# A two-layer relational graph convolution: node blocks of 256 instead of 512 in layer 1, a change of the gather table for each, and limits computed later

## The chip, the cores and the metric

The kernel runs on one core of a Trainium2 chip. The metric is device time in microseconds (us). Besides the timed runs there is one profiled execution, from which every view of the trace comes. Engines are named as in the profile: PE is TensorE (PEld its weight loads), DVE is VectorE, ACT is ScalarE, POOL is GpSimd, SP is SyncE. A "q" behind a name (SPq, ACTq, POOLq) is the engine's own queue, which issues DMAs and waits.

## The reference

12,500 nodes with 128 features each, and 200,000 edges, which come sorted by their destination node. An edge's type, one of 10, is the argmax of 10 of its 42 attributes. Each of two layers gathers the source rows, takes the mean for each pair of destination and type, multiplies it by the type's 128x128 matrix, and adds the root term and the bias:

```python
def _rgcn_layer(x, src, dst, edge_type, w_rel, root, bias):
    N = x.shape[0]
    seg = dst * NUM_REL + edge_type
    xs = x[src]
    sums = jax.ops.segment_sum(xs, seg, num_segments=N * NUM_REL)
    cnt = jax.ops.segment_sum(jnp.ones(seg.shape, x.dtype), seg, num_segments=N * NUM_REL)
    mean = (sums / jnp.maximum(cnt, 1.0)[:, None]).reshape(N, NUM_REL, -1)
    return jnp.einsum('nrd,rdo->no', mean, w_rel) + x @ root + bias
h = relu(_rgcn_layer(x, ..., w_rel1, root1, b1))
out = layernorm(x + _rgcn_layer(h, ..., w_rel2, root2, b2))
```

Layer 2 needs `h` of an edge's source, so in principle all of layer 1 comes first.

## The kernel before, in words

**Tiles, parts, blocks.** The edges are cut into NT = 1563 tiles of 128. Four tiles (QB) are a part; there are 391 parts. Layer 1 (`layer_1`, from L830) is one loop over the parts, its instructions in the order in which the Python code writes them (a manual schedule). For each tile POOL gathers 128 source rows by one indirect DMA (`gathered`, L747-750). DVE makes a one-hot matrix of 128 x 120 from the keys (`ones`, L757), ACT weights it (`weighted`, L752), PE multiplies it with the gathered rows (L976), and DVE adds the product to the sums `cc` (`sum_into`, L781) at a node offset that `offsets` loads from a row of limits, two parts later. `cc` is a ring over 1024 nodes for each layer. Since the edges are sorted, the sums of a block of nodes are complete after a certain tile, `done_after(k)`. Then `finish(k)` (L838) runs: `projected` (L730) multiplies the ten sums with the weight matrices on PE; one part later `rows_out` adds the bias, applies the relu (ACT) and turns the block on PE; two parts later `rows_kept` copies it to `hb` (ACT), and SP stores it to `hD`. `second` and `second_kept` write what the block already has of layer 2 to `T2`; `cleared` (L715) zeroes the ring; `fetch`, `turn` and `turned_kept` bring the next block's rows.

**The table.** From tile T0 = 166 on, a gather does not read `x` alone. It reads a row of `XH`, which is `x` beside `h`, if `h` is known for that node, and beside zero if not. So an edge whose source is in a finished block gets its layer 2 message in layer 1, at no further gather. There are two tables, `XH[0]` and `XH[1]`, used in turn. Blocks K0 to K1 (`KSEEN`, L49) each open an epoch: from a fixed tile on (`first_seen`, L124), a multiple of RT = 11 tiles behind T0 and at least READY = 6 parts after the part in which the block finishes, gathers read the other table, which holds this block too. `stored` (L743) writes the block's `hb` to the table that comes next, and, two parts into its epoch, to the other one (`todo_late`). `table_rows` (L819) fills the tables with `x` and zeros through the ACT queue, 13 pieces of 1024 rows for each table, at parts set in L931 to L934.

**Layer 2.** Edges whose source was not yet known are packed into NT2 tiles while layer 2 begins with tiles 0 to 165, which it gathers again from `hD`. `brought_together` (L1057) packs them, row by row: a row is 11 tiles, 1408 edges, and there are NR = 127 rows. How many places a row gets is fixed when the program is made: for a row whose epoch knows the nodes below b, 1408 x (1 - b/12500) plus 4.25 standard deviations (`groups`, `extents`, L131 to L147). `row_limits` (L386) puts b and the room of each row on the chip and `tile_limits` (L404) the nodes that a packed tile can reach; both are made of small DVE instructions and are only read in layer 2. Two walks over the packed tiles alternate, and layer 2 finishes its own blocks, the last of which ends the program.

**Buffers.** Gathers land in 7 buffers (GB). One holds 8 tiles while only `x` is gathered, 4 tiles with both halves from T0 on, and 8 tiles in layer 2. POOL can run that far ahead of PE.

**Prologue.** Before the loop the first 128 tiles' keys and weights are prepared. `places` (L350) computes each tile's node limit, in one DVE instruction for each block (L359), and `row_limits` is called there (L1033).

Of the kernel before, what the change touches and what calls it, by code (L numbers as in the profile page):

```python
# [20 lines left out]
P = 128  # L21
# [24 lines left out]
RT = 11  # L46
REACH = 560
SIGMAS = 4.25
KSEEN = (1, 21)  # L49
SPLIT = 63  # L50
LEAD = 40
LAST = 40
# [11 lines left out]
def rgcn_resnorm_kernel(ctx: ExitStack, tc: tile.TileContext, x, src, dst, attr, w_rel1, root1, b1,  # L64
# [16 lines left out]
    NPT = len(parts)  # L81
    CP = CT // QB
    NPAD = N + W
    starts = list(range(0, N - YB - 2 * P, YB))
    starts += list(range(starts[-1] + YB, N, P))
    lap = N // RN * RN
    assert lap in starts
    NBLK = len(starts)
# [261 lines left out]
    def places():  # L350
        off = keep.tile([NCH, CT], F32, name="off")
        early(0, nc.vector.tensor_tensor(off, b_i, even, op=ALU.subtract))
        b_f = keep.tile([NCH, CT], F32, name="b_f")
        lows = keep.tile([NCH, CT], F32, name="lows")
        early(0, nc.vector.memset(lows, 0.0))
        for size in (YB, P):
            for k in range(NBLK - 1):
                if done_after(k) < NT and starts[k + 1] - starts[k] == size:
                    early(0, nc.vector.scalar_tensor_tensor(lows, even, STEP * done_after(k) - 0.5, lows,  # L359
                                                            op0=ALU.is_gt, op1=ALU.add))  # L360
            if size == YB:
                early(0, nc.vector.tensor_scalar(lows, lows, float(YB // P), None, op0=ALU.mult))
# [12 lines left out]
        nc.vector.tensor_tensor(fl[:NCH], fl[:NCH], worst, op=ALU.max)  # L375
# [10 lines left out]
    def row_limits():  # L386

        nc.vector.memset(seen_below, float(starts[K0 + 1]))
        for i in range(3):
            nc.vector.memset(rooms[:, i:i + 1], float(groups[0][2 + i]))  # L390
        was_k, was = starts[K0 + 1], groups[0]
        for (k, r, _), now in zip(rows_of[1:], groups[1:]):
            more(seen_below, r, starts[k + 1] - was_k)
            for i in range(3):
                more(rooms[:, i:i + 1], r, now[2 + i] - was[2 + i])
            was_k, was = starts[k + 1], now

    NC2 = -(-NT2 // P)
    reach_of = [keep.tile([P, NC2], F32, name=f"reach{i}") for i in range(2)]
# [273 lines left out]
    def block_rows(a, k, l):  # L673
# [4 lines left out]
            nc.tensor.transpose(pr[:h, t, :], a[:, t * P:t * P + h], ident)  # L678
        if not l:
            nc.sync.dma_start(hT[:, n0:n0 + n], a[:, :n])  # L680
            hb = fin.tile([P, 4, C], F32, name="hb")
            for p, s in spans(k):
                nc.scalar.activation(hb[:p, s], pr[:p, s], AF.Copy)
            rows_dma(hb, hD, k, True)
# [145 lines left out]
    def layer_1():  # L830
# [2 lines left out]
        done = 0  # L833
        zps, ohs, xbs, fTs = {}, {}, {}, {}
        offs, row = None, None
        big = [k for k in range(NBLK) if block(k)[1] == YB]

        def finish(k, t):  # L838

# [21 lines left out]
            def rows_kept(_):  # L861
                pr = po.pop()
                hb = fin.tile([P, 4, C], F32, name="hb")
                for p, s in spans(k):
                    nc.scalar.activation(hb[:p, s], pr[:p, s], AF.Copy)
                rows_dma(hb, hD, k, True)
                if k <= K1:
                    first = 0 if k <= K0 else (k - K0) % 2
                    stored(hb, first, k)
                    if k < K1:  # L870
                        assert k <= K0 or t >= first_seen[k - 1]
                        when = t + 8 * QB if k < K0 else first_seen[k] + 2 * QB
                        todo_late.append((when, lambda t: stored(hb, 1 - first, k)))

# [14 lines left out]
                todo.at(t + 3 * u, lambda t: cleared(0, k, 1))  # L889
            if k < NBLK - 1:  # L890
                todo.at(t + (9 if k >= NBLK - 3 else 3) * u, second)
                todo.at(t + (9 if k >= NBLK - 3 else 5) * u, second_kept)
            else:
                todo.run(t)
                todo.run(END)
                todo.at(t, second)
                todo.at(t, second_kept)
            if both:
                w = 10 if k >= NBLK - 3 else 6
                todo.at(t + w * u, lambda t: cleared(1, k, 0))  # L900
                todo.at(t + (w + 1) * u, lambda t: cleared(1, k, 1))
            if k + 1 < NBLK - 1:
# [13 lines left out]
                    fTs[k + 1] = fin.tile([P, 4 * P], F32, name="fT")  # L916
                    nc.scalar.activation(fTs[k + 1][:, :n], pt[:, :n], AF.Copy)
                todo.at(t + u, fetch)
                w = 2 if k == NBLK - 3 else 5
                todo.at(t + w * u, turn)  # L920
                todo.at(t + (w + 1) * u, turned_kept)

# [4 lines left out]
        jobs = Later()  # L927
        for c in range(1, NCH):
            jobs.job(max(0, (c - 1) * CP - 3) * QB, prepared(c), QB)
        jobs.job(8 * QB, tile_limits(), 2 * QB)  # L930
        for b in range(2):  # L931
            for i, a in enumerate(range(0, N, 2 * YB)):
                n = i + b * 13
                jobs.at((1 + n * 3 // 2 if n < 22 else 1 + n * 2) * QB, lambda t, b=b, a=a: table_rows(b, a))  # L934
        for i, a in enumerate(range(0, NREL * RW, YB)):
            def wipe(t, a=a):
                m = min(YB, NREL * RW - a)
# [92 lines left out]
        pc = summed_up(0, same(0, kh, d), d, pc)  # L1030
    weights_out(0, weights_turned(0, [pc]))
    places()
    row_limits()  # L1033
    weights_in()
    in_order = ExitStack()
    in_order.enter_context(tc.manual_schedule())
# [652 lines left out]
```

## Time and profile before

| | us |
|---|---|
| median of 3 runs | 3094.66 (3094.16 to 3096.91) |
| the profiled execution's own time | 3098.4 |
| its span, first to last instruction | 3096.6 |
| gathers, all on POOL | 1397 from XH, 166 from x, 166 + 709 from hD |
| mean granted TensorE clock | 0.823 |

The page gives, for each group of instructions, the line, the engine, the operation and its operands, the count, the busy time, the mean of one in ns, and the idle time of the engine just before them with what ended it. "issue" there means that the profile shows nothing that the engine waited for. In views of windows each engine's busy time is followed by its count of instructions; behind them stand the granted clock, the busy share of the DMA engines and the GB/s. In a timeline a row has its start, its duration, the engine, the line and the operands.

### The profile page before, as it was taken

The numbers are of one execution on the slowest core, as the hardware profiler recorded it, in microseconds if no ns is written. First come the engines' busy times: TensorE is split into PE (matmuls) and PEld (weight loads), VectorE is DVE, ScalarE is ACT, GpSimd is POOL, SyncE is SP. The second block draws the span as 40 slices with busy tenths as digits, with TensorE's granted clock in tenths as the row PEclk, the third lists the DMA queues.
The fourth block names the chain that finished last, engine by engine and source line by source line (L and its number), as shares of the span: only waits on it lengthen the run. The fifth ranks groups of instructions, "written<-read, shape, count | busy, mean of one in ns | idle before, by whom it ended". The sixth has DMA issues, their size and how long they took to land.

```text
span 3096.6 us, 39943 instructions
## 1 busy us (share of the span) xinstructions
PE 2427.0 (78%) x10905; PEld 1805.4 (58%) x10905; DVE 1989.1 (64%) x5272; ACT 1292.9 (42%) x3006; POOL 2308.9 (75%) x2450
## 2 busy tenths in 40 slices
PE   2768887888888888888888899646577787777887
PEld 2546666566666566666666667545555555555665
DVE  7875746465656565555555554598677677677676
ACT  3543333333333333333333334322445555555453
POOL 7777777777777777777777777677777777777774
PEclk8768888888888878787888789856788999988888
DMA  7865445454545454545454444322222222222222
GB/s 210 233 204 173 143 124 159 120 163 123 163 119 163 121 162 124 162 123 162 123 161 124 127 121 120 101 58 63 60 70 74 73 74 74 74 74 73 74 73 59
DMA packets 260631, 371.57 MB, mean 120 GB/s; under 512 B 49654, under 2 KB 189467, under 8 KB 260404
## 3 DMA queue, kind: packets, MB, share of 16 engines
q0 software_dynamic: 100368, 251.49, 29.5%
q1 hardware_dynamic: 106339, 91.83, 9.6%
q10 hardware_dynamic: 53697, 25.62, 2.8%
q8 instruction: 94, 1.54, 0.2%
q14 instruction: 133, 1.09, 0.1%
HBM read 323.78 MB, written 57.76 MB: 123 GB/s over the span
## 4 chain that ended last, share of the span: by engine, by line
PE 37%; POOL 18%; issue 16%; DVE 13%; DMA 11%; ACT 3%; DVEq 1%; ACTq 0%; POOLq 0%; SPq 0%
POOL g L749 18%; PE pf L737 16%; DMA g<-XH,idxE 10%; PE zp L976 9%; PE zp L1479 8%; DVE cc L790 4%; DVE oh L766 2%; PE pf L740 1%; ACT cc L720 1%; ACT oh L755 1%; DVE cc L1157 1%; PE pf L1195 1%; DVEq L775 1%; DVE oh L763 1%; DVE go L1145 1%
## 5 line engine op out<-in xcount | busy, mean ns | idle before, releaser
L749 POOL DMA_INDIRECT g<-XH,idxE x1397 | 1321.7, 946 | 425.6 <-issue 383.9
L790 DVE TENSOR_TENSOR cc<-cc,zp 128x240 f32 (+16 forms) x2507 | 962.9, 384 | 719.7 <-PE zp L976 503.1
L976 PE MATMUL zp<-oh,g 128*128 128x120 f32 x5920 | 1053.4, 334 | 323.6 <-DMA g<-XH,idxE 230.5
L976 PEld LDWEIGHTS zp<-oh,g 128*128 128x128 f32 x5920 | 926.1, 236 | 482.4 <-issue 187.1
L749 POOL DMA_INDIRECT g<-hD,idxB x709 | 670.2, 945 | 216.1 <-issue 202.7
L755 ACT ACTIVATE oh<-oh,wE 128x120 f32<-128x120 f32 x1729 | 530.2, 383 | 640.8 <-DVE oh L763 557.3
L1479 PE MATMUL zp<-oh,g 128*128 128x120 f32 (+18 forms) x1888 | 514.8, 417 | 256.8 <-DVE cc L790 102.3
L737 PE MATMUL pf<-cc,w 128*128 128x256 f32 (+6 forms) x2120 | 691.4, 485 | 30.3 <-DVE cc L790 21.3
L1479 PEld LDWEIGHTS zp<-oh,g 128*128 128x128 f32 x1888 | 346.1, 230 | 401.8 <-issue 252.2
L737 PEld LDWEIGHTS pf<-cc,w 128*128 128x128 f32 x2120 | 411.8, 208 | 279.6 <-issue 205.0
L755 ACT ACTIVATE oh<-oh,wB 128x150 f32<-128x150 f32 (+18 forms) x778 | 342.6, 483 | 293.7 <-DVE oh L766 276.6
L766 DVE TENSOR_TENSOR oh<-go,keyB 128x480 f32<-128x480 f32 (+14 forms) x478 | 262.9, 550 | 132.8 <-PE zp L1479 131.6
L720 ACT ACTIVATE cc<-zero 128x2560 f32<-128x2560 f32 (+4 forms) x188 | 322.0, 1717 | 21.7 <-DVE cc L790 19.6
L763 DVE TENSOR_TENSOR oh<-bank,keyE 128x480 f32<-128x480 f32 x391 | 253.2, 648 | 0.0
L670 ACT ACTIVATE a<-pf,b 128x512 f32<-128x512 f32 (+1 forms) x27 | 17.3, 639 | 453.6 <-PE pf L740 453.6
L749 POOL DMA_INDIRECT g<-hD,idxE x166 | 158.4, 954 | 62.6 <-issue 46.6
L749 POOL DMA_INDIRECT g<-in_x_dram,idxE x166 | 157.0, 946 | 52.3 <-issue 47.2
L546 DVE TENSOR_TENSOR eqb<-bank,kh 128x1344 bf16<-128x1344 f32 (+2 forms) x65 | 100.5, 1549 | 2.3 <-PE pf L557 1.9
L555 PE MATMUL pf<-eqb,identb 128*128 128x512 bf16 (+2 forms) x130 | 64.7, 498 | 11.6 <-DVE eqb L546 11.4
L882 ACT ACTIVATE v<-pf,b 128x512 f32<-128x512 f32 (+2 forms) x29 | 18.0, 619 | 120.1 <-PE pf L740 100.5
L557 PE MATMUL pf<-eqb,identb 128*128 128x512 bf16 (+2 forms) x130 | 64.1, 493 | 0.0
L415 DVE SCALAR_TENSOR_TENSOR reach<-u,reach 128x6 f32<-128x6 f32 x252 | 42.2, 167 | 7.4
(235 smaller groups left out, 991.5 us busy)
## 6 DMA issues: line engine op xcount, KB each, us to landing
m<-in_edge_attr_dram SPq DMA_DIRECT2D x48, 672.0 KB
g<-XH,idxE POOLq DMA_INDIRECT x1397
XH<-in_x_dram ACTq DMA_DIRECT2D x24, 512.0 KB
XH<-zero ACTq DMA_DIRECT2D x24, 512.0 KB
g<-hD,idxB POOLq DMA_INDIRECT x709
XH<-hb SPq DMA_DIRECT2D x43, 256.0 KB
out_dram<-o SPq DMA_DIRECT2D x47, 128.0 KB
xb<-in_x_dram SPq DMA_DIRECT2D x23, 256.0 KB
```

Source lines behind the costliest of these rows:

```text
L546: nc.vector.tensor_tensor(eq[:p], kpP[:p, None, :R].to_broadcast([p, DB, R]), fore, op=ALU.is_equal)
L555: nc.tensor.matmul(pc[:p], identb[:p, :p], eq[:p, k:k + 4, L:], start=(d + k == 1), stop=False)
L557: nc.tensor.matmul(pc[:p], identb[:p, :p], back, start=False, stop=(d + k + 3 == L))
L720: nc.scalar.activation(cc[:, l, h * H:(h + 1) * H, o:o + n], zero[:, None, :n].to_broadcast([P, H, n]), AF.Copy)
L737: nc.tensor.matmul(po[:, :n], wsb[l][:, r, :], cc[:, l if ring is None else ring, r, o:o + n], start=(r == 0), stop=False)
L749: nc.gpsimd.indirect_dma_start(out=g[:, j * C:(j + n) * C], out_offset=None, in_=table, in_offset=bass.IndirectOffsetOnAxis(ap=idx, axis=0))
L755: nc.scalar.activation(s, s, AF.Copy, scale=w)
L763: nc.vector.tensor_tensor(o.rearrange("p (t m) -> p t m", m=m), cols[:, None, :m].to_broadcast([P, n, m]), keys[:, :, None].to_broadcast([ ...
L766: nc.vector.tensor_tensor(o.rearrange("p (t r n) -> p t r n", r=NREL, n=w), cols[:, None, :, :w].to_broadcast([P, n, NREL, w]), keys[:, :, ...
L790: nc.vector.tensor_tensor(s, s, z, op=ALU.add)
L976: nc.tensor.matmul(zp[:, a + l * KW:a + (l + 1) * KW], g[:, (slot[j] + l) * C:(slot[j] + l + 1) * C], oh[:, j * KW:(j + 1) * KW], start=Tr ...
L1479: nc.tensor.matmul(zp[:, j * m:(j + 1) * m], gt[:, b * C:(b + 1) * C], oh[:, j * m:(j + 1) * m], start=True, stop=True)
```

## The change

Blocks of layer 1 have 256 nodes instead of 512 (the last six stay at 128 and less). There are 52 instead of 29. Epochs are opened by blocks 3 to 43 instead of 1 to 21: the first still knows the nodes below 1024 and the last those below 11,264, but there are 41 instead of 21, and the known border moves by 256. `hb` becomes two buffers of half the size, in turn. The later steps of a finish move up by a part. `tile_limits` starts at part 80 instead of 8. `row_limits` leaves the prologue and becomes a job of the loop from part 180 on, eight DVE instructions every second part. The 26 pieces of the tables are issued at parts 1 + 3n/2 (rounded down) throughout; before, the last four of them stood at parts 45, 47, 49 and 51 (now 34, 35, 37 and 38). The second table's first piece comes second; the other pieces of the first table follow at once.

```diff
-KSEEN = (1, 21)
+BN = 2 * P
+KSEEN = (3, 43)
...
-    starts = list(range(0, N - YB - 2 * P, YB))
-    starts += list(range(starts[-1] + YB, N, P))
+    starts = list(range(0, N - YB - 2 * P, BN))
+    starts += list(range(starts[-1] + BN, N, P))
...
-        for size in (YB, P):
+        for size in (BN, P):
...
             was_k, was = starts[k + 1], now
+            yield 1
...
-                hb = fin.tile([P, 4, C], F32, name="hb")
+                hb = fin.tile([P, 2, C], F32, name=f"hb{k % 2}")
...
-                        assert k <= K0 or t >= first_seen[k - 1]
+                        assert k <= K0 or now + QB >= first_seen[k - 1]
...
-                todo.at(t + (9 if k >= NBLK - 3 else 5) * u, second_kept)
+                todo.at(t + (9 if k >= NBLK - 3 else 4) * u, second_kept)
...
-                w = 10 if k >= NBLK - 3 else 6
+                w = 10 if k >= NBLK - 3 else 5
...
-                w = 2 if k == NBLK - 3 else 5
+                w = 2 if k == NBLK - 3 else 4
...
-        jobs.job(8 * QB, tile_limits(), 2 * QB)
-        for b in range(2):
-            for i, a in enumerate(range(0, N, 2 * YB)):
-                n = i + b * 13
-                jobs.at((1 + n * 3 // 2 if n < 22 else 1 + n * 2) * QB, lambda t, b=b, a=a: table_rows(b, a))
+        jobs.job(80 * QB, tile_limits(), 2 * QB)
+        jobs.job(180 * QB, row_limits(), 2 * QB)
+        pieces = [(b, a) for b in range(2) for a in range(0, N, 2 * YB)]
+        pieces.insert(1, pieces.pop(len(pieces) // 2))
+        for n, (b, a) in enumerate(pieces):
+            jobs.at((1 + n * 3 // 2) * QB, lambda t, b=b, a=a: table_rows(b, a))
...
     places()
-    row_limits()
     weights_in()
```

More of the change, by code (lines that the diff above doesn't have):

```diff
@@ L360, in places @@
                                                             op0=ALU.is_gt, op1=ALU.add))
-            if size == YB:
-                early(0, nc.vector.tensor_scalar(lows, lows, float(YB // P), None, op0=ALU.mult))
+            if size == BN:
+                early(0, nc.vector.tensor_scalar(lows, lows, float(BN // P), None, op0=ALU.mult))
         early(0, nc.vector.tensor_scalar(lows, lows, float(P), None, op0=ALU.mult))
@@ L835, in layer_1 @@
         offs, row = None, None
-        big = [k for k in range(NBLK) if block(k)[1] == YB]
         def finish(k, t):
@@ L859, in rows_out, with rows_kept @@
                 po.append(pr)
-            def rows_kept(_):
+            def rows_kept(now):
                 pr = po.pop()
-                hb = fin.tile([P, 4, C], F32, name="hb")
+                hb = fin.tile([P, 2, C], F32, name=f"hb{k % 2}")
                 for p, s in spans(k):
```

## The prediction

> **What bounds the kernel now.** I read the page first, for the engine without gaps, then the groups of gathers, then single gathers in the timeline.
>
> ```profile
> span 3096.6 us, 39943 instructions
> PE 2427.0 (78%) x10905; PEld 1805.4 (58%) x10905; DVE 1989.1 (64%) x5272; ACT 1292.9 (42%) x3006; POOL 2308.9 (75%) x2450
> ...
> POOL 7777777777777777777777777677777777777774
> ...
> L749 POOL DMA_INDIRECT g<-XH,idxE x1397 | 1321.7, 946 | 425.6 <-issue 383.9
> ...
> L749 POOL DMA_INDIRECT g<-hD,idxB x709 | 670.2, 945 | 216.1 <-issue 202.7
> ...
> L749 POOL DMA_INDIRECT g<-hD,idxE x166 | 158.4, 954 | 62.6 <-issue 46.6
> L749 POOL DMA_INDIRECT g<-in_x_dram,idxE x166 | 157.0, 946 | 52.3 <-issue 47.2
> ```
>
> PE has more busy time than POOL, but its share changes from slice to slice; POOL shows a 7 in 38 of 40. Its work is 1397 + 709 + 166 + 166 = 2438 gathers of about 0.95 us, and the idle time before them is "issue": nothing that the profile shows held POOL up. The timeline of POOL's first and last gathers, on both sides of the only long gap, gives the pace:
>
> ```profile
> 4.15 1.11 POOL L749 DMA_INDIRECT g<-in_x_dram,idxE  x1 [1.98 <-DVE lane L333]
> ...
> 1957.81 0.95 POOL L749 DMA_INDIRECT g<-XH,idxE  x1 [0.30 <-issue]
> 1971.11 0.94 POOL L749 DMA_INDIRECT g<-hD,idxE  x1 [12.35 <-DMA hD<-hb]
> ```
> ```profile
> 3065.15 0.94 POOL L749 DMA_INDIRECT g<-hD,idxB  x1 [0.30 <-issue]
> ```
>
> Layer 1's 1563 gathers start within 1957.81 - 4.15 = 1953.7 us: 1.251 us each. Layer 2's 875 start within 3065.15 - 1971.11 = 1094.0 us: 1.252 us each. So the span is 4.2 (start) + 1953.7 + 13.3 (the step over the gap) + 1094.0 + 31.4 (tail behind the last gather) = 3096.6 us. **The count of gathers, at 1.25 us each, sets the time**; whatever makes POOL wait adds to it, and other work costs only if it does that. The profiled execution took 3098.4 us, 1.8 more than its span; the median of the runs, 3094.66, is 3.7 below that. I take the difference in the profile and subtract it from the median.
>
> **Fewer gathers: the gain.** NT2, the number of packed tiles, is arithmetic of the code. A row of 1408 edges is given 1408 x (1 - b/12500) places, b being the border of known nodes in its epoch. The border now moves by 256 and epochs open at a multiple of 11 tiles; where before an epoch of 66 tiles (tiles 232 to 297, with b = 1536) lasted, now b = 1536 holds for 33 and 1792 for the next 33. Worked out for all rows, 59 of the 127 get a border that is 256 higher, none a lower one; each saves 1408 x 256/12500 = 28.8 places: 1701 places, 13.3 tiles. With the margin and each walk rounded up, 504 + 205 = 709 tiles become 497 + 198 = 695. T0 stays 166, since the first epoch still begins behind node 1024. So 14 gathers of 709 go: 14 x 1.252 = **17.5 us**. The packed tiles' work falls with them: their one-hot columns go from 183,630 to 181,680 and bunches from 520 to 518, so nothing in layer 2 becomes heavier.
>
> **Twice as many finishes: nothing, under POOL's pace.** Layer 1 projects 46 blocks of 256 where it projected 23 of 512. From the groups by shape:
>
> ```profile
> L737 PE MATMUL pf<-cc,w 128*128 128x512 f32 x880 | 409.2, 622 | 0.0
> L737 PE MATMUL pf<-cc,w 128*128 128x256 f32 x880 | 224.0, 415 | 27.9 <-DVE cc L790 19.8 <-DVE cc L727 7.8
> ```
> ```profile
> L720 ACT ACTIVATE cc<-zero 128x2560 f32<-128x2560 f32 x88 | 204.6, 2326 | 0.0
> L720 ACT ACTIVATE cc<-zero 128x1280 f32<-128x1280 f32 x84 | 105.8, 1259 | 19.6 <-DVE cc L790 17.5 <-DVE dn L1253 2.1
> ```
>
> A projection has 20 rows, so the 512s were 44 projections of 409.2/44 = 9.3 us and a 256 (in layer 2) is 224.0/44 = 5.1 us. Instead of 44 there are 88: 88 x 5.1 - 409.2 = +39 us of PE. Clearing is 176 x 1.26 - 204.6 = +17 us of ACT. Projections also wait for DVE's sums, and there are twice as many. The 23 more blocks each store and load three more pieces on SP, of half the size, bytes as before. The cover is each engine's idle time beside POOL:
>
> ```profile
> 300.00:1900.00 1600.00, 1363.05 (x6370) 1000.82 (x6369) 913.79 (x2126) 606.86 (x1430) 1210.33 (x1280) 0.82 0.48 139
> 2000.00:2100.00 100.00, 46.92 (x199) 40.08 (x197) 95.97 (x172) 29.83 (x83) 75.93 (x80) 0.61 0.23 60
> ```
> (columns: PE, PEld, DVE, ACT, POOL busy and counts, granted clock, DMA share, GB/s.) In the first window PE is idle for 237 of 1600 us, DVE for 686, ACT for 993. I take 0; without cover PE's 39 us would be the price.
>
> **Twice as many epochs: a deadline each.** The first gather of an epoch must wait until `hb` has landed in the table, 20 times more. The tightest before, by the code, are 16 tiles between the part that stores (block 13: tile 920) and the epoch (936); after the change the smallest is 16 again, three times (blocks 16, 27 and 38). What 16 tiles leave, from the timelines of SP's queue and of POOL, for the first epoch and for block 13's:
>
> ```profile
> 203.81 0.50 SPq L632 DMA_DIRECT2D XH<-hb  x1
> ```
> ```profile
> 211.76 0.95 POOL L749 DMA_INDIRECT g<-XH,idxE  x1 [0.30 <-issue]
> ```
> ```profile
> 1166.66 0.51 SPq L632 DMA_DIRECT2D XH<-hb  x1
> ```
> ```profile
> 1174.75 0.94 POOL L749 DMA_INDIRECT g<-XH,idxE  x1 [0.30 <-issue]
> ```
>
> About 8 us from issue to use both times, and POOL kept its 0.30. A store of `hb` has one landing in the chain of waits, and a store in the busiest stretch another:
>
> ```profile
> 1967.73 2.44 DMA hD<-hb
> ```
> ```profile
> 149.12 6.14 DMA T<-v
> ```
>
> Both are below 8. Before `hb` there is now one projection of 5.1 us, not 9.3, so the store comes some 4 us earlier against its epoch. Three epochs last only 22 tiles; there the store of the block before, which SP holds until the old epoch's gathers are done, stands behind this block's. Bounds: 0, and, if that second store is a part (4 x 1.25 = 5 us) late and takes the slow landing, 5 + 6.1 - 8 = 3 us at each of the three, 9 us. I take 0, nearest to the two rows of 8 us.
>
> **The tables filled sooner.** The last four pieces move from parts 45 to 51 to parts 34 to 38, just ahead of the first epoch (block 3 stores at part 37, as block 1 did). What the queue does under load, and what room there is:
>
> ```profile
> 140.00:180.00 40.00, 22.13 (x96) 18.13 (x95) 31.30 (x118) 21.42 (x59) 30.25 (x33) 0.64 1.08 342
> 180.00:220.00 40.00, 29.48 (x115) 19.61 (x115) 29.27 (x106) 17.26 (x43) 30.25 (x33) 0.76 0.41 115
> 220.00:260.00 40.00, 27.18 (x145) 22.51 (x144) 30.59 (x85) 11.26 (x36) 30.25 (x33) 0.80 0.66 198
> ```
> ```profile
> 158.23 4.92 ACTq L825 DMA_DIRECT2D XH<-zero  x1
> ```
>
> At 140 to 180 us the DMA engines are full and one issue holds ACT for 4.92 us; the next 40 us are at 0.41 and take what 220 to 260 shows above that, 0.25 at most. That gives about 0.66, not full. Low end 0; high end: three pieces ahead of `hb` on ACT, each holding it for 4.92, less the 8 us of room: 7 us. I take 0, by the window's 0.41. What is behind a held ACT is the weights of the next parts and `hb`, and behind `hb` the first epoch's gather.
>
> **Limits moved.** Each epoch's step of `row_limits` is eight tiny DVE instructions:
>
> ```profile
> L383 DVE TENSOR_SCALAR some<-place 128x1 f32<-128x1 f32 x86 | 12.4, 145 | 0.8
> L384 DVE TENSOR_TENSOR rooms<-rooms,some 128x1 f32<-128x1 f32 x60 | 9.1, 152 | 0.4
> L359 DVE SCALAR_TENSOR_TENSOR lows<-even,lows 13x128 f32<-13x128 f32 x28 | 7.8, 277 | 0.0
> ```
>
> The prologue loses 20 x 8 x 0.15 = 24 us of them and gains 23 x 0.28 = 6.4 us in L359. POOL does not feel either: its seven buffers hold 56 gathers, so it first needs one back at 4.15 + 56 x 1.25 = 74 us, and PE's products begin far earlier:
>
> ```profile
> 45.98 4.00 PE zp L976 x20
> 49.98 11.74 issue
> 61.72 1.18 PE zp L976 x4
> ```
>
> In the loop, 40 x 8 x 0.15 = 48 us of DVE over 80 parts (400 us) lie in DVE's idle time of 43%; a step delays sums by 1.2 us every 10 us, and behind the sums wait the projections and the next products' PSUM; between these and POOL lie seven buffers, 28 gathers or 35 us. `tile_limits` only moves. Value 0.
>
> One rule speaks against that. The Trainium skill ("SBUF — State Buffer", section "SBUF: two separate sides") says that DVE and GpSimd share a port pair under an exclusive lock, so that some DVE instructions keep GpSimd from writing the descriptors of its DMAs. No run here shows such a lock: in 2000 to 2100 us DVE is busy for 95.97 us, and POOL still issues 80 gathers, against 1280/16 = 80 per 100 us in the long window.
>
> **Gap and tail** stay: the last six blocks, which make the gap, are the same, and layer 2's last blocks have the same sizes and distance from the end. I allow 3 us either way.
>
> **Sum:** -17.5 + 0. In the profile 3098.4 - 17.5 = 3080.9; as a median 3094.66 - 17.5 = **3077 us**.
>
> **Rivals.**
>
> *Part of it given back at a few epochs.* The filling holds up the first epoch (up to 7 us) or the short ones stall (up to 9 us): 3078 to 3093; around 3085 with half of each. For it: DMA is full shortly before, and ACT carries both the pieces and `hb`. Against it: 8 us of room, the shorter projection.
>
> *`hb` becomes late at every epoch: slower.* PE is late by the 39 us and by longer waits for DVE, and the store's lead falls from 8 us to below its landing of 2.4. From there each of 41 epochs stalls POOL, and PE does not catch up because POOL waits for it in turn. It decides from a loss of 5.6 us at the end of a finish; 2 us beyond that at 40 epochs are +80: 3157 us, and half a microsecond each takes the whole gain. For it: the clock (0.82) and PE's 85% in layer 1. Against it: 237 us idle against 39.
>
> *DVE holds POOL up.* The extra DVE work (24 us in `row_limits`, 6 in L359), if each microsecond stopped POOL, gives 3077 + 30 = 3107 us. The window at 96% DVE speaks against it. It is what the skill's lock would do.
>
> *It doesn't do what it says.* The packing falls to another limit, or gaps eat all of the gain: 3094. NT2 is fixed when the program is made, so only gaps can do this.
>
> **How the numbers follow.** Forecast (3071 to 3082): 0.75. Given back in part (3082 to 3088): 0.12. Nothing gained: 0.06. Late `hb`: 0.05. DVE: 0.02. The range goes from 3077 - 3 (tail) - 3 (gap) = 3071 to 3088, where the half-given-back cases lie, and leaves out about 0.15. A measurement of this kernel can tell about 0.2%, 6 us, from no change: faster (below 3088.5) 0.87, the same 0.06, slower 0.07.
>
> **What would show it.** Right: 695 gathers g<-hD,idxB; POOL at 1.25 us throughout; one gap of about 12 us behind hD<-hb; PE's projections at about 450 us in layer 1; a tail of 31 us. Wrong: waits of POOL for XH<-hb or XH<-zero around 212 us or at epochs; a period above 1.25 us between 900 and 1300 us, where `row_limits` now stands.

## The result, and the profile after

The changed kernel takes **3113.24 us** (median of 5 runs, 3108.35 to 3115.32); the kernel before takes 3094.66 (5 runs beside them, 3094.07 to 3097.15). The ratio is 1.0054, with a 95% interval of 1.0039 to 1.0068. The forecast was 3077, so the kernel is slower where it was forecast to be faster. The profiled execution of the changed kernel took 3108.35 us, with a span of 3106.5.

The page of the changed kernel, first its heads and POOL's slices, then the four groups of gathers (lines are one or two higher than before, so L749 is now L751):

```profile
span 3106.5 us, 42362 instructions
...
PE 2368.2 (76%) x11861; PEld 1949.5 (63%) x11861; DVE 2031.1 (65%) x5465; ACT 1301.6 (42%) x3177; POOL 2295.8 (74%) x2436
...
POOL 7777777777777777777777777677777777777772
...
L751 POOL DMA_INDIRECT g<-XH,idxE x1397 | 1321.2, 946 | 425.6 <-issue 384.8
L751 POOL DMA_INDIRECT g<-hD,idxB x695 | 657.3, 946 | 215.9 <-issue 195.3
L751 POOL DMA_INDIRECT g<-hD,idxE x166 | 158.8, 957 | 61.7 <-issue 46.0
L751 POOL DMA_INDIRECT g<-in_x_dram,idxE x166 | 156.9, 945 | 52.2 <-issue 47.9
```

The 14 gathers are gone: 695 instead of 709. But POOL's last slice shows a 2 where it showed a 4: POOL ends earlier and the kernel goes on without it. The timeline of POOL's first and last gathers gives the terms of the prediction's sum:

```profile
4.12 1.11 POOL L751 DMA_INDIRECT g<-in_x_dram,idxE  x1 [1.95 <-DVE lane L334]
...
1957.12 0.95 POOL L751 DMA_INDIRECT g<-XH,idxE  x1 [0.30 <-issue]
1969.45 0.94 POOL L751 DMA_INDIRECT g<-hD,idxE  x1 [11.38 <-PE pf L742]
```
```profile
2482.81 0.94 POOL L751 DMA_INDIRECT g<-hD,idxB  x1 [2.01 <-PE zp L1480]
```
```profile
2685.34 0.94 POOL L751 DMA_INDIRECT g<-hD,idxB  x1 [2.29 <-PE zp L1480]
```
```profile
3050.91 0.94 POOL L751 DMA_INDIRECT g<-hD,idxB  x1 [0.30 <-issue]
```

| term, us | before | forecast | after |
|---|---|---|---|
| start | 4.2 | 4.2 | 4.1 |
| layer 1's gathers | 1953.7 | 1953.7 | 1953.0 |
| step over the gap | 13.3 | 13.3 | 12.3 |
| layer 2's gathers | 1094.0 | 1076.5 | 1081.5 |
| tail behind the last gather | 31.4 | 31.4 | 55.6 |
| span | 3096.6 | 3079.1 | 3106.5 |

Layer 1 went as forecast. The miss lies in layer 2: **24.2 us in the tail**, and 5 us in the gathers, of which 3.7 us are the two waits for PE above (2.01 and 2.29 us, where 0.30 is usual). Both say that PE falls behind the gathers. What it waits for is in its waits. First the kernel before, in layer 1 (300 to 1900 us) and in layer 2 (2200 to 3050 us), then the changed kernel in layer 2; a row has the waiting engine and line, what it waited for, the us in total, the count and the longest:

```profile
PE zp L976 <- DMA g<-XH,idxE: 209.8, 305, 4.1
PE zp L976 <- DVE cc L790: 5.2, 10, 0.7
```
```profile
PE zp L1479 <- DVE cc L790: 66.8, 43, 7.7
PE zp L1479 <- issue: 61.2, 26, 3.1
...
PE zp L1479 <- DMA g<-hD,idxB: 7.6, 7, 3.5
```
```profile
PE zp L1480 <- DVE cc L792: 122.9, 67, 9.3
...
PE zp L1480 <- DMA g<-hD,idxB: 5.9, 5, 1.9
```

In layer 1 PE waits for gathers, so POOL sets the pace there. In layer 2 of the kernel before it hardly ever did (7 times): it waited for DVE's sums (66.8 us), and in the changed kernel it waits for them almost twice as long. What DVE does in that time shows in its timeline, with the products that wait behind it:

```profile
2289.08 0.42 DVE L768 TENSOR_TENSOR oh<-go,keyB 128x260 f32<-128x260 f32 x1
2290.95 0.43 DVE L792 TENSOR_TENSOR cc<-cc,zp 128x260 f32 x1 [1.46 <-issue]
```
```profile
2291.63 1.35 PE L1480 MATMUL zp<-oh,g 128*128 128x260 f32 x4 [1.54 <-DVE cc L792]
```

The idle 1.46 us before a sum has no releaser, because DVE's own queue is busy: it loads node offsets into registers (`offsets`), and the load that starts at 2288.6 us takes 2.15 us. These loads, by their line, between 2200 and 2450 us and over the whole run, before and after (durations in ns: least, median, greatest; then the starts of the first and the last):

```profile
L775 DVEq TENSOR_LOAD <-rowB x25: 593/596/606, 2223.0 to 2441.1; - x25
```
```profile
L777 DVEq TENSOR_LOAD <-rowB x23: 594/1841/2195, 2224.9 to 2443.0; - x23
```
```profile
L775 DVEq TENSOR_LOAD <-rowB x89: 591/597/902, 2223.0 to 3070.5; - x89
```
```profile
L777 DVEq TENSOR_LOAD <-rowB x88: 310/599/2195, 2224.9 to 3085.3; - x88
```

The median load took 0.60 us, now 1.84 us in that stretch; over the run the loads add up to 54.0 us before and 86.0 us after. The code says which are slow: layer 2's second walk starts at packed tile UX, which was 504, a multiple of 8, and is 497 now. Every load of that walk, 25 in all and 14 of them in this stretch, now starts one word behind a multiple of 8.

### The profile page after: what moved, and what is told of

Its sections match the earlier page's. It is cut to its first block, busy times and chain, and to the rows that moved or that the text cites. A ratio compares the mean times of both kernels' runs of the same rounds, so it can differ in the third digit from the quotient of the medians.

```text
span 3106.5 us, 42362 instructions
## 1 busy us (share of the span) xinstructions
PE 2368.2 (76%) x11861; PEld 1949.5 (63%) x11861; DVE 2031.1 (65%) x5465; ACT 1301.6 (42%) x3177; POOL 2295.8 (74%) x2436
## 4 chain that ended last, share of the span: by engine, by line
PE 30%; POOL 22%; issue 19%; DVE 14%; DMA 10%; ACT 2%; DVEq 1%; ACTq 0%; POOLq 0%; SPq 0%
POOL g L751 22%; PE pf L739 13%; DMA g<-XH,idxE 9%; PE zp L978 8%; PE zp L1480 6%; DVE cc L792 5%; DVE oh L768 2%; PE pf L742 1%; DVE cc L1158 1%; DVEq L777 1%; ACT cc L722 1%; ACT oh L757 1%; DVE oh L765 1%; DVE st L703 1%; DVE go L1146 1%
## 5 line engine op out<-in xcount | busy, mean ns | idle before, releaser
L751 POOL DMA_INDIRECT g<-XH,idxE x1397 | 1321.2, 946 | 425.6 <-issue 384.8
L792 DVE TENSOR_TENSOR cc<-cc,zp 128x240 f32 (+13 forms) x2500 | 959.8, 384 | 777.8 <-PE zp L978 388.2
L978 PE MATMUL zp<-oh,g 128*128 128x120 f32 x5920 | 983.2, 318 | 370.5 <-DMA g<-XH,idxE 206.8
L978 PEld LDWEIGHTS zp<-oh,g 128*128 128x128 f32 x5920 | 866.5, 222 | 487.2 <-issue 184.8
L751 POOL DMA_INDIRECT g<-hD,idxB x695 | 657.3, 946 | 215.9 <-issue 195.3
L739 PE MATMUL pf<-cc,w 128*128 128x256 f32 (+4 forms) x3000 | 732.1, 405 | 18.9 <-DVE cc L792 15.1
L1480 PE MATMUL zp<-oh,g 128*128 128x120 f32 (+23 forms) x1874 | 507.3, 415 | 284.4 <-DVE cc L792 156.4
L739 PEld LDWEIGHTS pf<-cc,w 128*128 128x128 f32 x3000 | 610.4, 215 | 121.1 <-DVE cc L792 22.5
L1480 PEld LDWEIGHTS zp<-oh,g 128*128 128x128 f32 x1874 | 338.9, 227 | 430.9 <-issue 271.0
L757 ACT ACTIVATE oh<-oh,wB 128x150 f32<-128x150 f32 (+23 forms) x771 | 339.1, 482 | 296.5 <-DVE oh L768 269.4
L722 ACT ACTIVATE cc<-zero 128x1280 f32<-128x1280 f32 (+3 forms) x274 | 336.6, 1231 | 85.3 <-DVE cc L792 81.5
L768 DVE TENSOR_TENSOR oh<-go,keyB 128x480 f32<-128x480 f32 (+20 forms) x476 | 260.3, 547 | 115.1 <-PE zp L1480 113.6
L751 POOL DMA_INDIRECT g<-hD,idxE x166 | 158.8, 957 | 61.7 <-issue 46.0
L751 POOL DMA_INDIRECT g<-in_x_dram,idxE x166 | 156.9, 945 | 52.2 <-issue 47.9
L883 ACT ACTIVATE v<-pf,b 128x256 f32<-128x256 f32 (+2 forms) x52 | 23.9, 459 | 361.4 <-PE pf L742 333.2
```

The costliest lines, as they stand in the source:

```text
L722: nc.scalar.activation(cc[:, l, h * H:(h + 1) * H, o:o + n], zero[:, None, :n].to_broadcast([P, H, n]), AF.Copy)
L739: nc.tensor.matmul(po[:, :n], wsb[l][:, r, :], cc[:, l if ring is None else ring, r, o:o + n], start=(r == 0), stop=False)
L751: nc.gpsimd.indirect_dma_start(out=g[:, j * C:(j + n) * C], out_offset=None, in_=table, in_offset=bass.IndirectOffsetOnAxis(ap=idx, axis=0))
L757: nc.scalar.activation(s, s, AF.Copy, scale=w)
L768: nc.vector.tensor_tensor(o.rearrange("p (t r n) -> p t r n", r=NREL, n=w), cols[:, None, :, :w].to_broadcast([P, n, NREL, w]), keys[:, :, ...
L792: nc.vector.tensor_tensor(s, s, z, op=ALU.add)
```

## The experiments

Two things were to be settled: whether those loads make the loss (theory A), and why the tail was open to it, though POOL was to set the time. Later the second question became theory P (the count of gathers sets the end of layer 2 too) against theory C (the chain of DVE and PE does, and POOL only runs ahead of it).

**1. The loads of the changed kernel at multiples of 8 words.** A first short load, then eights:

```diff
-                            m = min(GB2, (UX, NT2)[l] - t)
+                            m = min(GB2 - t % GB2, (UX, NT2)[l] - t)
```

> The kernel after, but the first load of node offsets in layer 2's second walk takes 7 tiles instead of 8, so that all later loads of that walk begin at a multiple of 8 words (504, 512, ...) as they did before the change; nothing else differs. Theory A (the offset loads, 1.85 us instead of 0.60 us each since the walk begins at tile 497, make layer 2 late): all loads at about 0.6 us, no wait of POOL in layer 2 beyond its 0.3 us, last gather at about 3046 us, tail of about 31 us, median 3077 us (3073 to 3083). Theory B (the finer widths or the order of layer 2's finishes make it late): the tail stays above 50 us and the median at 3105 to 3115 us.

Measured: 3089.86 us against 3095.33 for the kernel before; ratio 0.9982 (0.9973 to 0.9991). One expression takes 23 us back. The 88 loads sum to 55.2 us:

```profile
L777 DVEq TENSOR_LOAD <-rowB x88: 311/596/1657, 2223.4 to 3065.7; - x88
```

POOL no longer waits in layer 2; its last gather is at 3046.2 of 3088.0 us, so the tail is 41.8 us, not 31. The loads made the loss, but of the gain of 17.5 only 5.5 is there, and the 3077 us that theory A expected were not reached. PE still waits for DVE's sums more than before, 101.0 us between 2200 and 3050 us where the kernel before has 66.8:

```profile
PE zp L1480 <- DVE cc L792: 101.0, 55, 9.2
```

**2. The fault alone, in the kernel before.** Its second walk starts at 504; here its loads start one word later.

```diff
-                            m = min(GB2, (UX, NT2)[l] - t)
+                            m = min(GB2 - (t - l) % GB2, (UX, NT2)[l] - t)
```

> The kernel before, but the second walk's first load takes 1 tile, so that all later loads of that walk begin at a multiple of 8 words plus 1 (505, 513, ...); nothing else differs. Theory A: 25 loads of about 1.85 us instead of 0.60, 31 us more on DVE's queue in layer 2, a tail of 50 us or more and 3110 to 3125 us. Theory B: 3095 us, the same as before.

Measured: 3116.3 us, ratio 1.0066 (1.0051 to 1.0081). Its loads between 2200 and 2450 us:

```profile
L775 DVEq TENSOR_LOAD <-rowB x24: 316/1842/2067, 2221.1 to 2432.8; - x24
```

They are as slow as the changed kernel's, with no other part of the change present, and the time rises by 21 us. The last gather stays at 3065.7 us; the tail goes from 31.4 to 48.5 us. Theory A holds from both sides.

**3. Loads at four words behind a multiple of 8**, in the changed kernel:

```diff
-                            m = min(GB2, (UX, NT2)[l] - t)
+                            m = min(GB2 - (t + 4 * l) % GB2, (UX, NT2)[l] - t)
```

> The kernel after, but the second walk's first load takes 3 tiles, so that later loads begin at a multiple of 8 words plus 4 (500, 508, ...): 16 bytes off a multiple of 32. If loads must begin at a multiple of 32 bytes to be fast (A1): 1.85 us each and 3108 to 3115 us, as after. If a multiple of 16 bytes is enough (A2): 0.6 us each and 3077 us. Theory B: 3108 to 3115 us with loads of 0.6 us.

Measured: 3086.31 us, ratio 0.9966 (0.9954 to 0.9978); 89 loads, 54.9 us, median 0.60. So four words (16 bytes) are alignment enough for the loads. The time is not the 3077 us of that expectation; the tail is 38.8 us.

**4. Blocks of 256, but epochs as before.** On top of experiment 1, only every second block opens an epoch; the block's second store reads its rows back from `hD`:

```diff
-    for k in range(K0, K1 + 1):
+    for k in range(K0, K1 + 1, 2):
...
+                    e = max(0, (k - K0 + 1) // 2)
+                    first = e % 2
...
```

> The kernel after with the loads mended, but only every second block opens an epoch, so that the 21 epochs, the borders and the 709 packed tiles are those of before, while layer 1 still finishes 52 blocks; the second store of a block to the tables reads its rows back from hD instead of from the buffer. If twice as many finishes cost nothing under POOL's pace, and the gain of the change is the 14 gathers alone: 3094 us (3090 to 3098), 17.5 us above the run with the loads mended and 41 epochs. If finishes cost something, it is above 3098 us by that.

Measured: 3098.47 us, ratio 1.0009 (0.9999 to 1.0018), with 709 packed tiles, the last gather at 3066.0 and a tail of 30.2 us. That is half a microsecond above the range expected. Twice as many finishes cost at most 6 us by the interval, and 0 lies in it; the last gather is 0.8 us later than before. Nothing here speaks against the step that took them for nothing.

**5. Gathers left out of the kernel before.** The purest test of "the count of gathers sets the time": in layer 2, 14 gathers are not made, and everything else stays.

```diff
+                        if second and (t0 + j) % 50 == 25:
+                            gs[second, t0 + j] = g, (made - 1) % GQ
+                            continue
```

> The kernel before, where 14 of the 709 gathers of layer 2's packed tiles (one in 50) are not made: their products read the rows of the gather before them, so these tiles contribute wrong rows and all other work stays. Theory P (the count of gathers sets the end of layer 2 as well): the last gather is 14 x 1.25 = 17.5 us earlier, the tail stays at 31 us, the time falls by 17.5 us to about 3077. Theory C (in layer 2 the chain of DVE and PE sets the end and POOL only runs ahead of it): the last gather is 17.5 us earlier, but the tail grows to 42 to 48 us, PE's products lag their gathers by 10 us or more beyond what they do before, and the time falls by 0 to 6 us, to 3089 to 3095.

> The kernel before without 14 of the gathers of layer 2's packed tiles, as twice before on chips on which the kernel before took 3964 us (there it was 0.5 to 0.6% faster); now for a chip on which the kernel before takes 3095. Theory P: the last gather 17.5 us earlier, tail 31 us, about 3077. Theory C: the last gather 17.5 us earlier, tail 42 to 48 us, 3089 to 3095.

Measured, on a chip on which the kernel before takes 3096.12 us: 3096.27 us, ratio **0.9997** (0.9988 to 1.0006). Nothing is gained. POOL did end 17 us earlier; its last gather:

```profile
3048.50 0.94 POOL L749 DMA_INDIRECT g<-hD,idxB  x1 [0.31 <-issue]
```

The tail took all of it: 3096.3 - 3048.5 = 47.8 us. PE's waits for DVE between 2200 and 3050 us are those of the kernel before, 65.2 us for 66.8:

```profile
PE zp L1482 <- DVE cc L790: 65.2, 43, 8.1
```

Theory P falls.

**6. Less DVE work in the changed kernel.** On top of experiment 3, the last step of the layer norm goes from DVE to ACT:

```diff
-            nc.vector.tensor_scalar(o[:h, t, :], v[:h, t, :], mv[:h, t, 0:1], rstd[:h, t:t + 1],
-                                    op0=ALU.subtract, op1=ALU.mult)
+            nc.scalar.activation(o[:h, t, :], v[:h, t, :], AF.Identity, bias=sh[:h, t:t + 1], scale=rstd[:h, t:t + 1])
```

with `sh`, the mean times -rstd, made by one small DVE instruction for each span of rows.

> The changed kernel with the loads at multiples of four words and the last step of the layer norm on ACT, for a chip on which the kernel before takes 3095 us (on the others, where it takes 3954 to 3964, the move changed 4012 to 4022 at most). Theory C: tail 30 to 33 us, 3077 to 3081. Rival, the chain runs through ACT too: as without the move, 3084 to 3088 beside a kernel before of 3095, tail about 39 us. Theory P: the same as that rival.

Measured: **3076.57 us** (3075.42 to 3077.74) against 3095.86, ratio 0.9939 (0.9925 to 0.9953). It is the fastest of all, ahead of both kernels. Its last gather and its new ACT work:

```profile
3046.70 0.94 POOL L753 DMA_INDIRECT g<-hD,idxB  x1 [0.30 <-issue]
```
```profile
L713 ACT ACTIVATE o<-v,sh,rstd 128x128 f32<-128x128 f32 (+2 forms) x101 | 44.2, 485 | 20.8 <-DVE sh L711 20.8
```

POOL ends where it did in experiment 3 (3046.2); the tail is 26.9 us instead of 38.8. ACT has 44 us more to do and it does not show: of DVE, ACT and PE, DVE's work is what the end hung on.

**7. The same move in the kernel before.** Does the move bring its 10 us alone?

> The kernel before with the last step of the layer norm on ACT, for a chip on which the kernel before takes 3095 (on one where it takes 3963 the move changed nothing). If the shorter chain only lets the count of gathers set the end: last gather at 3065 as before, tail 27 instead of 31 us, 3089 to 3092; the change is then worth 14 to 17 us. If the move gives its 9 to 10 us by itself: 3085 to 3087.

Measured: 3095.60 us against 3096.44, ratio 0.9997 (0.9988 to 1.0006): again nothing, not even the 3 to 6 us that were expected from the tail. Now POOL holds the end. The last gather stays, and PE waits for gathers more often, 23 times where it was 7:

```profile
3065.79 0.94 POOL L751 DMA_INDIRECT g<-hD,idxB  x1 [0.31 <-issue]
```
```profile
PE zp L1481 <- DMA g<-hD,idxB: 12.7, 23, 0.8
```

Experiments 5, 6 and 7 together show two bounds of almost the same length in layer 2. Shorten POOL's alone, nothing; shorten DVE's alone, nothing; shorten both, 19 us (experiment 6's kernel has the rest of the change too, but its layer 2 starts within 1.2 us of the kernel before's). How far PE is behind POOL shows the same. The numbers are worked out from the traces: the start of a bunch's first product less the end of its last gather, in us, at the bunch nearest to that gather of layer 2. A bunch is the tiles whose products share one `zp`. Bunches side by side differ by up to 6 us.

```
gather of layer 2             200  400  600  850   tail
before                         24   26   18   11   31.4
before, loads shifted (2)      21   37   37   29   48.5
after                          26   59   46   36   55.6
after, loads at 8 words (1)    25   41   31   21   41.8
after, loads at 4 words (3)    26   39   28   19   38.8
256, epochs as before (4)      23   25   16   10   30.2
after (3), norm on ACT (6)     22   26   11    6   26.9
before, norm on ACT (7)        19   16    1    2   27.9
```

All are at 19 to 26 us at gather 200. That backlog builds up while the packed tiles are made: by the same working it is 8 to 10 us for products at about 2105 us and 30 to 34 us at about 2190. In between lie PE's waits for DVE and 110 matmuls of the packing itself (L1195, from 2140.6 to 2178.6 us). Before, it shrinks until the end, and 11 us are left. In the changed kernel it grows between gathers 200 and 400, where 15 of the 25 slow loads are, and the rest of layer 2 takes only part of it back. With the loads mended (1 and 3) it still grows there, from 25 or 26 us to about 40; no run shows why.

The tail follows from it. The last bunch's first product starts 12.6 us behind the end of its last gather before, 37.8 after, 8.7 in experiment 6 and 7.3 in experiment 7; in all eight kernels the tail is 18 to 21 us longer than that.

**Runs on other chips.** Eleven runs fell on chips on which the kernel before takes 3954 to 3964 us, and say little of the above. They are told by kernel, each with what was expected.

*Experiment 5's kernel*, whose first expectation stands there, had 0.9948 (0.9928 to 0.9968) and, in a second run, 0.9937 (0.9912 to 0.9962). There the gathers left out do save time, 21 and 23 us:

> The kernel before, where 14 of the 709 gathers of layer 2's packed tiles (one in 50) are not made; their products read the rows of the gather before them, so these tiles contribute wrong rows, and all other work stays. The same kernel was run once on a chip on which the kernel before took 3964 us. Theory P (the count of gathers sets the end of layer 2 as well): the last gather is 14 x 1.25 = 17.5 us earlier, the tail stays at 31 us, the time falls to about 3077. Theory C (in layer 2 the chain of DVE and PE sets the end and POOL only runs ahead of it): the last gather is 17.5 us earlier, the tail grows to 42 to 48 us, and the time falls by 0 to 6 us, to 3089 to 3095.

*Fourteen gathers more* had 1.0061 (1.0040 to 1.0082), 1.0079 (1.0053 to 1.0106) and 1.0103 (1.0073 to 1.0133). This kernel ran on no other chip, so what they cost where the kernel before takes 3095 us is not known:

```diff
+                        if second and (t0 + j) % 50 == 25:
...
+                            gathered(g, made % GQ, hD, idx, 1)
+                            made += 1
```

> The kernel before with 14 gathers more in layer 2 (one behind every 50th packed tile, with that tile's indices, into a slot of the ring that nothing reads). Theory P: +17.5 us, about 3112, tail 31 us. Theory C: PE's products lag the gathers by 11 us at the end of before, against 4 us where they follow at once, so the first 7 us or so are taken up by that lag: the time rises by 8 to 13 us, to 3103 to 3108, and the tail shrinks to 22 to 27 us.

> The kernel before with 14 gathers more in layer 2 (one behind every 50th packed tile, into a slot of the ring that nothing reads); run before on the chip where the kernel before took 3964 us. Theory P: +17.5 us, about 3112, tail 31 us. Theory C: PE's products lag the gathers by 11 us at the end of before, against 4 us where they follow at once, so the lag takes up the first 7 us or so: the time rises by 8 to 13 us, to 3103 to 3108, and the tail shrinks to 22 to 27 us.

> The kernel before with 14 gathers more in layer 2 that nothing reads, now for a chip on which the kernel before takes 3095 us. Theory P: 3112, tail 31 us. Theory C: leaving 14 out gained nothing, so the chain has no slack below the gathers; adding 14 delays each gather by up to 17.5 us, of which the lag of PE (11 us at the end of before, 4 us where it follows at once) takes up about 7: 3103 to 3108, tail 22 to 27 us.

*Experiment 6's kernel* had 1.0139 (1.0115 to 1.0162), 1.0144 (1.0117 to 1.0172) and 1.0156 (1.0132 to 1.0180); *experiment 3's* 1.0132 (1.0101 to 1.0163) and 1.0136 (1.0114 to 1.0158). Both are slower there than the kernel before, and hardly differ. One place where they lose is the epochs. In these five traces POOL waits 156 to 242 us for stores of `hb` into the table, 26 to 31 times; in the six of kernels with the epochs of before it waits 115 to 130 us, 10 or 11 times; in experiments 1 to 7 above 0.6 us at most. So on these chips `hb` does come late at most of the 41 epochs, as one of the prediction's rivals had it. What they expected:

> The changed kernel with the loads at multiples of four words (as in the run before of that kind: 3086, tail 39 us), and the last step of the layer norm moved from DVE to ACT, as a scale and a shift: DVE loses 101 x 0.37 = 37 us of L710 and gains 54 tiny products of about 0.16 us = 9 us, so 28 us less of DVE, all in layer 2; ACT gains 101 instructions. The count of gathers stays. Theory P: only the last block's own chain changes: within 2 us of 3086. Theory C: the lag of PE falls through layer 2, as its chain is shorter: tail 30 to 33 us and a time of 3077 to 3081, which is what the prediction had forecast for the change itself.

> The changed kernel with the loads at multiples of four words, and the last step of the layer norm moved from DVE to ACT, as a scale and a shift; run before on the chip where the kernel before took 3964 us. DVE loses 101 x 0.37 = 37 us of L710 and gains 54 tiny products of about 0.16 us = 9 us: 28 us less, all in layer 2. Theory P: within 2 us of the run without the move. Theory C: the lag of PE falls through layer 2, as its chain is shorter: tail 30 to 33 us, a time of 3077 to 3081. If the move costs the chain more on ACT than it saves on DVE, it is slower than the run without.

> The changed kernel with the loads at multiples of four words, as it stood at 3086 us with a tail of 39 us, beside the three others on their chip, so that the move of the norm can be read against it. Both theories: within 5 us of 3086 where the kernel before takes 3095.

> The changed kernel with the loads at multiples of four words and the last step of the layer norm on ACT (28 us less of DVE work in layer 2), now for a chip on which the kernel before takes 3095 us. That the 14 gathers left out of the kernel before changed nothing there (ratio 0.9997) speaks for theory C, the chain of DVE and PE. Theory C: a shorter chain moves the end without any gather removed: tail 30 to 33 us, 3077 to 3081. Rival, the chain runs through ACT as well (a one-hot goes from DVE over ACT to PE): what DVE saves ACT adds, 3084 to 3088 with a tail of about 39 us. Theory P is within 2 us of the run beside it without the move.

> The changed kernel with the loads at multiples of four words, beside the run with the norm's last step on ACT, so that the two can be compared on one chip: 3086 within 4 us, tail 39 us.

*Experiment 7's kernel* had 0.9995 (0.9980 to 1.0010):

> The kernel before with the last step of the layer norm on ACT, for a chip on which the kernel before takes 3095. With it the changed kernel (loads at multiples of four words) fell from 3086 to 3077. If the shorter chain only lets the count of gathers set the end, the 14 more gathers of the kernel before hold it up: last gather at 3065 as before, tail 27 instead of 31 us, 3089 to 3092, and the change is then worth its 14 to 17 us. If the move gives its 9 to 10 us by itself, whatever the count of gathers: 3085 to 3087.

## Why the prediction was wrong, point by point

**"The count of gathers, at 1.25 us each, sets the time": the step that failed.** It holds in layer 1. In layer 2 POOL is as steady, but it is only ahead: with 56 gathers of buffer it can be 70 us ahead of PE before it waits once. A producer that never waits is the bound only if its consumer waits for it. The prediction read POOL's 7s and its "issue", and did not ask PE: in layer 2 PE's waits for gathers were 7 of the kernel before's, and those for DVE's sums 43. Experiment 5 measured what the step took for 17.5 us: 0.

**"Other work costs only if it makes POOL wait"** failed with it. In the changed kernel 32 us of slow loads cost 23 us (experiment 1), of which POOL shows 5.

**"So nothing in layer 2 becomes heavier": the overlooked term.** One-hot columns and bunches were counted. That UX goes from 504 to 497, and with it the first word of every load in a walk, was not. Nor did DVE's work fall with the gathers. Its sums and one-hots of layer 2, and the steps that set each packed tile's width, one for every change of width, before and after:

```profile
L790 DVE TENSOR_TENSOR cc<-cc,zp 128x120 f32 (+18 forms) x944 | 353.2, 374 | 103.3 <-PE pf L737 35.2 <-DMA row<-b_i 15.3 <-ACT cc L720 14.3
L766 DVE TENSOR_TENSOR oh<-go,keyB 128x480 f32<-128x480 f32 (+14 forms) x478 | 262.9, 550 | 132.8 <-PE zp L1479 131.6 <-PE pf L1230 0.3
...
L1242 DVE TENSOR_SCALAR bB<-place 128x1 f32<-128x1 f32 x19 | 2.9, 152 | 0.5
```
```profile
L792 DVE TENSOR_TENSOR cc<-cc,zp 128x120 f32 (+23 forms) x937 | 350.1, 374 | 129.3 <-PE pf L739 35.6 <-issue 32.7 <-DMA row<-b_i 14.8
L768 DVE TENSOR_TENSOR oh<-go,keyB 128x480 f32<-128x480 f32 (+20 forms) x476 | 260.3, 547 | 115.1 <-PE zp L1480 113.6
...
L1243 DVE TENSOR_SCALAR bB<-place 128x1 f32<-128x1 f32 x30 | 4.6, 153 | 0.8
```

Sums and one-hots fall by 5.7 us, from 616.1 to 610.4, but more epochs mean more changes of width: 30 steps instead of 19, and each has an addition behind it. In the windows of layer 2 (from 1969 us to the end before, from 1968 us to the end in experiment 3) DVE is busy for 818.0 us before and 818.2 us in experiment 3. So DVE's work stayed as it was while the gathers fell by 17.5 us. Which part of the chain gave the 5.5 and 9 us of experiments 1 and 3 is not shown. The idle time "issue" before the sums, now 32.7 us, is the slow loads: it is 28.5 us in experiment 2 and 7.7 in experiment 1, where the loads are fast.

**"Gap and tail stay."** The gap did (12.3 us), though by the profile its wait now ends with PE's L742 and not with the store of `hb`. The tail did not, by 24.2 us. It is no constant: it is 18 to 21 us plus PE's lag at the last bunch.

**14 fewer packed tiles: right.** 695, as counted, and 1081.5 us of gathers instead of 1094.0, 5 us more than forecast, for PE's sake. With the norm on ACT in both kernels the change, its loads at multiples of four words, takes 3095.60 to 3076.57 us, 19.0 (the two ran beside kernels before of 3096.44 and 3095.86), and layer 2's gathers take 3046.70 - 1970.00 = 1076.7 us there, against 1076.5 forecast. Where the chain leaves room, the sum was about right.

**Twice as many finishes: right.** Layer 1's gathers took 1953.0 us. The 256 wide projections are 2640 matmuls now:

```profile
L739 PE MATMUL pf<-cc,w 128*128 128x256 f32 x2640 | 671.4, 415 | 17.6 <-DVE cc L792 14.2 <-DVE cc L729 3.3
```

Two thirds of them, 88 of 132 projections, are layer 1's: 447.6 us, the forecast 450. PE stayed under POOL's pace, and experiment 4 agrees.

**Twice as many epochs, and the table: right, where the kernel before takes 3095 us.** No epoch made POOL wait there. At the first one the store and the first gather of the new table, from SP's queue and POOL:

```profile
200.94 1.38 SPq L634 DMA_DIRECT2D XH<-hb  x1
```
```profile
211.59 0.94 POOL L751 DMA_INDIRECT g<-XH,idxE  x1 [0.30 <-issue]
```

10.7 us from issue to use, where 8 were forecast. The DMA engines are full a little earlier and at 0.57 in the window for which 0.66 was worked out (the last three columns are the clock, the DMA share and GB/s):

```profile
140.00:180.00 40.00, 26.60 (x117) 21.24 (x115) 21.79 (x63) 20.13 (x59) 30.25 (x33) 0.72 1.10 355
180.00:220.00 40.00, 26.36 (x111) 21.35 (x112) 27.43 (x76) 15.65 (x46) 30.25 (x33) 0.67 0.57 168
```

**Limits moved: right, but not tried alone.** Layer 1's gathers neither gained nor lost by it.

**The rivals.** None was what happened on these chips. "DVE holds POOL up" gave 3107 us, near the measured time, by a mechanism that the trace refutes. In 300 to 1900 us, where the moved limits lie, the changed kernel's POOL (the fifth engine column) has 1281 instructions, one more than before:

```profile
300.00:1900.00 1600.00, 1315.62 (x7294) 1140.71 (x7292) 994.34 (x2671) 619.24 (x1596) 1210.05 (x1281) 0.85 0.48 140
```

And its two waits of 2 us in layer 2 are for PE. A right number with a wrong path would have carried nothing over. The rival that was missing is plain from the waits of PE: the chain of DVE and PE is the bound of layer 2, and the gathers saved are worth nothing there.

## What to carry to other kernels

Ask the consumer, stage by stage, before you name the producer the bound: a producer with deep buffers looks steady whether it leads or not, and only a consumer that waits for it proves that it sets the time. Where two bounds are of one length, shortening one shows nothing, so try both together before you drop either. When a size that the code computes changes, follow every address that starts from it, not only the counts.

## What the runs showed of the hardware

**A load of registers depends on where it starts.** Eight words took a median of 0.60 us from a start at a multiple of 4 words (experiments 1 and 3), and 1.84 us, up to 2.2, from one word behind a multiple of 8 (the changed kernel, experiment 2). The first and last loads of the second walk are shorter, and from such a start they took 0.75 us for three words (experiment 3), 0.98 for four (experiment 2), 1.42 for six (the changed kernel) and 1.66 for seven (experiment 1): about 0.22 us for each word more. It looks as if such words were loaded one by one; other starts were not tried, and why it is so stays open.

The Trainium skill ("DMA: Bandwidth & Descriptors", section "Latency and other measured facts") gives a floor of about 600 ns for a `tensor_load`. The aligned loads of eight words here take that, 596 to 599 ns in the median, but it is no floor: loads of a single word took 0.31 us (in the changed kernel, and 0.32 in experiment 2). The Trainium skill ("Runtime: NRT & Kernel Launch", section "Instruction fetch mechanics") also puts a load at about 200 ns for each register, even in bulk. By that figure an estimate for eight is 1.6 us. The misaligned loads are near it with 1.84 us, the aligned ones far below.

**The same kernels on some chips take 28 to 31% longer.** There the engines stop before instructions that wait for nothing the profile shows, and the granted clock is 0.75 to 0.78, not 0.82 to 0.84. Rows of POOL and of PE's weight loads, of experiment 3's kernel on such a chip and then in its run of 3086 us:

```profile
PEld zp L978 <- issue: 744.6, 584, 24.1
POOL g L751 <- issue: 732.4, 2170, 8.8
```
```profile
POOL g L751 <- issue: 677.9, 2225, 0.3
...
PEld zp L978 <- issue: 184.0, 126, 18.2
```

PE's weight loads stop 584 times for 744.6 us, not 126 times for 184.0, and the longest such stop of POOL is 8.8 us, not 0.3. The 867 us that the kernel before loses there are 22 ns for each of its 39,943 instructions; experiment 3's kernel executes 2420 more, 53 us by that rate, and was 51 to 58 us slower than the kernel before there. That fits a cost for each instruction, but no run was made to test it, and POOL's longer waits at the epochs (above) are a rival of the same size.
